# The gate products of a gated linear attention stage, four row groups at once instead of two and two

## The chip, the core and the metric

The kernel runs on one core of one Trainium2 chip. A core has five engines with queues of their own: TensorE (PE; its weight loads are shown as PEld), VectorE (DVE), ScalarE (ACT), GpSimd (POOL) and SyncE (SP, which here issues most DMA transfers). TensorE reads SBUF and writes PSUM, which has eight banks of 128 partitions by 512 float32 values. The engines meet at semaphores. The metric is the device time of one execution in microseconds (us); times are medians of several runs.

## The reference

For 16 batch entries of 256 tokens with 256 features, four layers are added to x one after the other, each on a layernormed x and scaled by the tanh of a scalar gate: a latent cross attention over a context of 77 tokens, a top-2 mixture of experts, a masked cross attention, and the layer that this change is about, a gated linear attention. Cut to what matters here:

```python
q1, k1, v = x @ Wq * scale, x @ Wk, x @ Wv              # 8 heads of 64
q2, k2 = x @ Wqa @ Wqb * scale, softmax(x @ Wka @ Wkb)
gk1 = log_sigmoid(x @ Wg1a @ Wg1b + bg1) / 16           # log decays, per token and feature
gk2 = log_sigmoid(x @ Wg2a @ Wg2b + bg2) / 16
e = softmax(x @ We); idx = top_1(e)                     # 4 experts
o = chunk_gla(q1, k1, v, gk1) + sum over experts of chunk_gla(q2 * e, k2 * e, v, gk2 * mask)
o = o * rsqrt(mean(o * o) + eps) * norm_w * silu(x @ Wga @ Wgb)
out = x + tanh(g_ffn[1]) * (o @ Wo)
```

The two log decays gk1 and gk2 come from products with a contracted dimension of 17 only: 16 low-rank features and a row of ones for the bias.

## The kernel before

The kernel computes everything in float32. Its first two stages (the cross attentions and the experts) are not touched. The last stage, `stage3_fast` (L1530), holds the work of a block, one batch entry b of 256 tokens in two halves of 128 (`tokens(i)`), in four steps, one for each pair of heads: step p belongs to block p // 4, and m = p % 4 is the pair. The order of instructions is written out by hand; after the first part of the stage each engine runs its instructions in program order. The loop (L1905) runs 64 steps, and in each:

- `shares` (den: sums of the second keys' exponentials, on PE into a general bank), `masked(p - 1, 1)` (DVE: four multiplications of the second score product of the step before), `gated` in odd steps (DVE, u), `shares_end` (DVE reads den: `second`, then the reciprocal kden),
- `keys_queries(p + 1)` (PE, kq: keys first, tile wk, then queries, tile wq),
- the tables `middle` and `rest` (what else is due in this step, mostly for the next block), then `decays(p + 1)` (PE gq and gz, ACT ee), then the table `late`,
- `products(p, 0)` (PE, the first score product: sc from f), `masked(p, 0)` (DVE, at from sc and amask), `factors` (DVE, f), the table `by_rows`, `second(p + 1)` (PE, the other halves of gq and gz; ACT, e2), `factors_second` (POOL k, DVE q), the table `logs`,
- `products(p, 1)` (PE, the second score product: sc from q and k) and `values(p - 1)` (PE, o).

A general bank comes from `bank(name)` (L1540): in the loop it is a rotation of two PSUM banks, so a tile waits until the readers of the tile two requests earlier are done. The score products have a tile of two banks to themselves, sc, and only one such tile: the second product of a step waits until DVE has masked the first.

For the next block b + 1, step 0 has `lows` (L1588; PE into a general bank, then two DVE operations make low, whose partitions 64 to 80 and 96 to 112 hold the 17 rows for the two gates), `route_logits` (rt) and, for its own block, `outgates` (zg, with DVE's copy zs in `outgates_end`). Steps 1 and 2 have `gates(b + 1, 0)` and `gates(b + 1, 1)` (L1631): for one half of the tokens two products, out of 17 rows at partitions 64 and 96, each into a general bank, and two Exp by ACT. So they stand between the two score products of their step. `gate_logs` makes the logarithm and `steepest` a maximum for a later check; `decays` reads the result lg four steps on. `scaled` (ms on PE, Ln and Exp on ACT, oT on POOL) normalizes the finished half of the block before, and `project` (proj) in step 2 multiplies it with Wo.

In the profile all matrix products of this stage have line L1548, all transposes L1551, and all DVE, ACT and POOL operations L50; the tile names tell them apart.

Of the kernel before, what the change touches and what calls it, by code (L numbers as in the profile page):

```python
# [10 lines left out]
F32 = mybir.dt.float32  # L11
I32 = mybir.dt.int32
AF = mybir.ActivationFunctionType
ALU = mybir.AluOpType
# [3 lines left out]
P = 128  # L18
B, S, D = 16, 256, 256
# [4 lines left out]
V_LN1G, V_LN1B, V_LN2G, V_LN2B, V_QB, V_KB, V_NW, V_ONE, V_GATE, V_N = 0, 2, 4, 6, 8, 10, 12, 13, 14, 18  # L24
# [49 lines left out]
def layers(ctx: ExitStack, tc: tile.TileContext, t, out, check):  # L74
    nc = tc.nc
# [6 lines left out]
    def const(name, shape, dtype=F32):  # L82
        return cp.tile(list(shape), dtype, tag=name, name=name)
# [33 lines left out]
    vec = const("vec", [P, V_N])  # L117
# [44 lines left out]
    dve3, act3, pool3 = free = [Pinned(tc, x, False) for x in (nc.vector, nc.scalar, nc.gpsimd)]  # L162
# [622 lines left out]
    def w3_load(name, shape, src=None):  # L785
        x = c3(name, shape)
        src = t[src or name]
        weights.append((x, src if len(src.shape) == len(shape) else src.rearrange("(k p) f -> p k f", p=P)))
        return x
# [3 lines left out]
    lbg = w3_load("lbg", [P, 512])  # L793
# [736 lines left out]
    def stage3_fast(early_bank):  # L1530

        with ExitStack() as sx:
# [3 lines left out]
            def of(b):  # L1536

                return w1 if b % 2 else w0

            def bank(name):  # L1540
                return pss.tile([P, 512], F32, tag="ps", name=name) if pss else early_bank(name)

            def tokens(i):
                return slice(i * P, (i + 1) * P)


            def matmul(*a, **k):
                tc.keep_in_program_order(nc.tensor.matmul(*a, **k))  # L1548
# [3 lines left out]

            halves = w1.tile([P, P], F32, tag="halves", name="halves")
            nc.sync.dma_start(out=halves, in_=t["halves"])
            wo = w1.tile([P, 4, D], F32, tag="wo", name="wo")

            hots = [w1.tile([P, 2, 36], F32, tag=f"hot{n}", name=f"hot{n}") for n in range(2)]
# [3 lines left out]
            xn, xnT, low, lg, hT, em, am = {}, {}, {}, {}, {}, {}, {}  # L1561
# [26 lines left out]
            def lows(b):  # L1588

                low[b] = of(b).tile([P, 2, S], F32, tag="low", name="low")  # L1590
                ps = bank("low")
                for c in range(2):
                    for k in range(2):
                        matmul(ps[:, c * S:(c + 1) * S], la[:, k, c * P:(c + 1) * P], xnT[b][:, k, :],
                                         start=k == 0, stop=k == 1)
                dve3.tensor_copy(low[b][:, 0, :], ps[:, :S])
                dve3.tensor_scalar(low[b][:, 1, :], ps[:, S:], vec[:, V_ONE:V_ONE + 1], None, ALU.add)

            e_, den_, z_ = {}, {}, {}

# [30 lines left out]
            def gates(b, i):  # L1631

                if i == 0:
                    lg[b] = of(b).tile([P, 2, 2, 512], F32, tag="lg", name="lg")
                for n, (lo, hi) in enumerate(((64, 81), (96, 113))):
                    ps = bank("z")
                    matmul(ps, low[b][lo:hi, 1, tokens(i)], lbg[lo:hi, :], start=True, stop=True)
                    act3.activation(lg[b][:, i, n, :], ps, AF.Exp, scale=-1.0)

            def gate_logs(b, i):  # L1640
                act3.activation(lg[b][:, i], lg[b][:, i], AF.Ln, bias=1.0)
# [57 lines left out]
            def place(p):  # L1699
                b, m = p // 4, p % 4  # L1700
                return b, m, slice(m * P, (m + 1) * P)

            ee, kq, gq, gz, e2, fq, fk, rd, at, o = {}, {}, {}, {}, {}, {}, {}, {}, {}, {}

            def keys_queries(p):
                b, m, cols = place(p)
                kq[p] = psu.tile([P, 512], F32, tag="kq", name="kq")
                for w, lo in ((wk3, 0), (wq3, S)):
                    for k in range(2):
                        matmul(kq[p][:, lo:lo + S], w[:, k, cols], xnT[b][:, k, :],  # L1710
                                         start=k == 0, stop=k == 1)
# [21 lines left out]
            def shares(p):  # L1733

                ps = bank("den")
                for i in range(2):
                    matmul(ps[:, 2 * i:2 * i + 2], e2[p][:, tokens(i)], halves[:, 0::64],
                                     start=True, stop=True)
                z_[p, "den"] = ps

            def shares_end(p):
                ps = z_.pop((p, "den"))
                rd[p] = st.tile([P, 4], F32, tag="kden", name="kden")
                dve3.tensor_tensor(check["second"], check["second"], ps[:, :4], ALU.max)
                dve3.reciprocal(rd[p], ps[:, :4])
                pool3.tensor_tensor(check["rsum"][:, :4], check["rsum"][:, :4], rd[p], ALU.add)
# [27 lines left out]
            def masked(p, n):  # L1774
                b, m, cols = place(p)
                ps = z_.pop((p, n, "sc"))
                a = w2.tile([P, 2, 384], F32, tag=f"at{n}", name=f"at{n}")
                if n == 0:
                    at[p] = a
                    dve3.tensor_tensor(a, ps[:, :, :384], bc(amask, [P, 2, 384], 1), ALU.mult)  # L1780
                else:
                    r = rd.pop(p)
                    for lo, hi, i in ((0, S, 0), (S, 3 * P, 1)):
                        for j in range(2):
                            dve3.scalar_tensor_tensor(a[:, j, lo:hi], ps[:, j, lo:hi], r[:, 2 * i + j:2 * i + j + 1],
                                                           am[b][:, lo:hi], ALU.mult, ALU.mult)
                    if p == last - 1:
                        at[p] = a
                        return
                    pool3.tensor_tensor(at[p], at[p], a, ALU.add)  # L1790
# [25 lines left out]
            def gated(b, mp):  # L1816
                ps = z_.pop((b, mp, "o"))
                dve3.tensor_tensor(u_[b][:, 2 * mp:2 * mp + 2, :].rearrange("p m s -> p (m s)"), ps,
                                        gw[b][:, 2 * mp:2 * mp + 2, :].rearrange("p m s -> p (m s)"), ALU.mult)
# [36 lines left out]
            def warm():  # L1856

                ps = bank("warm")
                for _ in range(2):
# [2 lines left out]

            start = {0: [(turn, 1)], 2: [(turn_hot, 1)]}
            copies = {2: [(turned_hot, 1)]}
            middle = {0: [(lows, 1)], 1: [(scaled, -1, 1)], 2: [(pairs, 1)], 3: [(scaled, 0, 0)]}

            rest = {0: [(bias, 2)], 1: [(route, 1)], 2: [(steepest, 1, 0), (stats, 2)], 3: [(steepest, 1, 1)]}
            late = {2: [(project, -1)], 3: [(vals, 1)]}
            behind_mask = {0: [(route_logits, 1)], 3: [(norm, 2)]}
            by_rows = {0: [(outgates, 0, 0)], 1: [(gates, 1, 0)], 2: [(gates, 1, 1)], 3: [(outgates, 0, 1)]}  # L1870
            logs = {0: [(route_sums, 1), (outgates_end, 0, 0)], 1: [(gate_logs, 1, 0)], 2: [(gate_logs, 1, 1)],
                    3: [(outgates_end, 0, 1)]}

            def run(steps, p):
                for f, d, *a in steps.get(p % 4, ()):
                    if 0 <= p // 4 + d < B:
                        f(p // 4 + d, *a)
# [16 lines left out]
            w1 = sx.enter_context(tc.tile_pool(name="f3w1", bufs=1, reuse_waits="tile"))  # L1894
            w2 = sx.enter_context(tc.tile_pool(name="f3w2", bufs=2, reuse_waits="tile"))
            psa = sx.enter_context(tc.tile_pool(name="f3psa", bufs=1, space=PSUM, reuse_waits="tile"))
# [8 lines left out]
            for p in range(last):  # L1905
                run(start, p)
                shares(p)
                if 0 < p:
                    masked(p - 1, 1)
                run(copies, p)  # L1910
                if 1 < p and p % 2 == 1:
                    gated((p - 2) // 4, (p - 2) % 4 // 2)
                shares_end(p)
                if p + 1 < last:
                    keys_queries(p + 1)
                run(middle, p)
                run(rest, p)
                if p + 1 < last:
                    decays(p + 1)
                run(late, p)  # L1920
                products(p, 0)
                masked(p, 0)
                run(behind_mask, p)
                if p + 1 < last:
                    factors(p + 1)
                run(by_rows, p)
                if p + 1 < last:
                    second(p + 1)
                    factors_second(p + 1)
                run(logs, p)  # L1930
                products(p, 1)
                if 0 < p:
                    values(p - 1)
                    if p % 2 == 0:
                        squares((p - 1) // 4, (p - 1) % 4 // 2)

            b, p = B - 1, last - 1
# [126 lines left out]
```

## Time and profile before

| | |
|---|---|
| runs | 1928.58, 1929.67, 1936.73 us; median 1929.67 |
| profiled execution | 1930.67 us, of which the span from the first to the last instruction is 1928.8 |
| granted TensorE clock | 0.998 of full speed |
| gate products (z), both token halves, 16 blocks | 128 records, median 588 ns, from 1249.3 to 1865.1 us |
| Exp of a gate (ACT, 128x512) | 64, median 593 ns |
| last stage's loop, one block | 40.70 us |

In the timeline a row gives start, duration, engine, line, operation, the tiles out<-in, the shape, and how many instructions are merged in it; in brackets stands how long the engine was idle before and what ended that. A float32 product shows two records. Records of different row groups of the array overlap, and a record's duration has a tail in which the next one already runs, so how long a product holds PE is read from start to start.

### The profile page before, as it was taken

The numbers are of one execution on the slowest core, as the hardware profiler recorded it, in microseconds if no ns is written. First come the engines' busy times: TensorE is split into PE (matmuls) and PEld (weight loads), VectorE is DVE, ScalarE is ACT, GpSimd is POOL, SyncE is SP. The second block draws the span as 40 slices with busy tenths as digits, with TensorE's granted clock in tenths as the row PEclk, the third lists the DMA queues.
The fourth block names the chain that finished last, engine by engine and source line by source line (L and its number), as shares of the span: only waits on it lengthen the run. The fifth ranks groups of instructions, "written<-read, shape, count | busy, mean of one in ns | idle before, by whom it ended". The sixth has DMA issues, their size and how long they took to land.

```text
span 1928.8 us, 34998 instructions
## 1 busy us (share of the span) xinstructions
PE 1901.3 (99%) x14028; PEld 1323.0 (69%) x14028; DVE 1091.0 (57%) x2637; ACT 870.4 (45%) x1803; POOL 993.5 (52%) x895
## 2 busy tenths in 40 slices
PE   8999999999999999999999999999999999999997
PEld 5666666666766667666787766667777777777775
DVE  3335555455554555544474488865666656666654
ACT  3433334443444434443343588744444444444442
POOL 3644756557565575755635656124444444444433
PEclk9999999999999999999999999999999999999999
DMA  9300000000000000000078733000000000000000
GB/s 337 140 1 3 14 11 14 7 11 14 11 14 9 8 14 9 12 10 9 12 250 250 191 49 49 5 1 6 7 7 6 12 6 7 6 6 7 12 7 14
DMA packets 54028, 75.04 MB, mean 39 GB/s; under 512 B 10096, under 2 KB 43744, under 8 KB 53344
## 3 DMA queue, kind: packets, MB, share of 16 engines
q1 hardware_dynamic: 41568, 55.92, 8.6%
q0 software_dynamic: 12288, 16.79, 4.3%
q8 instruction: 113, 1.85, 0.4%
q14 instruction: 59, 0.48, 0.1%
HBM read 39.14 MB, written 33.55 MB: 38 GB/s over the span
## 4 chain that ended last, share of the span: by engine, by line
PE 95%; DVE 2%; ACT 1%; POOL 1%; issue 0%; DMA 0%; SPq 0%; ACTq 0%; POOLq 0%; DVEq 0%
PE o L50 13%; PE qk L50 13%; PE sc L50 10%; PE v L50 9%; PE proj L50 7%; PE kq L1548 6%; PE sc L1548 5%; PE ex L50 3%; PE gq L1548 3%; PE v L1548 3%; PE proj L1548 3%; PE o L1548 3%; PE gz L1548 2%; PE z L1548 2%; PE den L1548 1%; PE low L1548 1%
## 5 line engine op out<-in xcount | busy, mean ns | idle before, releaser
L50 POOL TENSOR_SCALAR rs<-mv 128x2 f32<-128x2 f32 (+1 forms) x92 | 17.6, 191 | 463.5 <-DVE mv L50 459.8
L50 ACT ACTIVATE qk<-qk 128x256 f32<-128x256 f32 x128 | 49.3, 385 | 343.7 <-PE qk L50 343.6
L50 ACT ACTIVATE e<-sc 111x1024 f32<-111x1024 f32 x192 | 182.2, 1021 | 16.9 <-PE sc L50 16.9
L50 PE MATMUL sc<-qk 64*111 64x256 f32 x1536 | 182.2, 383 | 0.0
L50 PE MATMUL o<-e,v 111*32 111x256 f32 x3072 | 177.5, 379 | 0.0
L50 PE MATMUL v<-wkv,kvT 128*111 128x512 f32 x384 | 169.3, 597 | 0.6 <-DVE kvT L50 0.6
L50 DVE RECIPROCAL rd<-o 128x256 f32<-128x256 f32 x64 | 112.3, 1755 | 99.7 <-PE o L50 99.7
L50 PEld LDWEIGHTS sc<-qk 64*111 64x111 f32 x1536 | 132.1, 172 | 52.9 <-issue 29.0
L50 POOL TENSOR_TENSOR esum<-esum,es 111x512 f32<-111x512 f32 x128 | 163.0, 1274 | 10.0
L50 PE MATMUL qk<-kvT,wkv 128*128 128x333 f32 x512 | 164.3, 443 | 0.0
L50 POOL TENSOR_TENSOR es<-e 111x1024 f32<-111x1024 f32 x64 | 151.2, 2363 | 23.9 <-ACT e L50 22.7
L50 POOL TENSOR_TENSOR k<-e,ee 128x256 f32<-128x256 f32 x64 | 46.8, 732 | 221.9 <-ACT e L50 221.9
L50 POOL TENSOR_TENSOR es<-es,e 111x1024 f32<-111x1024 f32 x64 | 150.4, 2349 | 5.0
L50 PEld LDWEIGHTS o<-e,v 111*32 111x32 f32 x3072 | 99.8, 110 | 66.0
L50 DVE COPY qk<-qk 128x333 f32<-128x333 f32 x128 | 64.6, 504 | 124.5 <-ACT qk L50 123.0
L50 PE MATMUL qk<-kvT,wq 128*128 128x256 f32 x512 | 134.3, 385 | 0.0
L50 PEld LDWEIGHTS v<-wkv,kvT 128*111 128x111 f32 x384 | 67.1, 178 | 91.6 <-issue 90.1
L50 DVE TENSOR_TENSOR at<-sc,amask 128x768 f32<-128x768 f32 x64 | 61.3, 957 | 115.9 <-PE sc L1548 100.6
L50 POOL TENSOR_TENSOR at<-at,at 128x768 f32<-128x768 f32 x63 | 113.9, 1808 | 25.0 <-DVE at L50 15.2
L50 POOL DMA_INDIRECT x<-rows_out,pos x64 | 100.1, 1564 | 37.3 <-issue 15.7
L50 PEld LDWEIGHTS qk<-kvT,wkv 128*128 128x128 f32 x512 | 97.2, 190 | 30.0
L50 PEld LDWEIGHTS qk<-kvT,wq 128*128 128x128 f32 x512 | 94.3, 189 | 34.0 <-issue 13.2
(247 smaller groups left out, 4128.8 us busy)
## 6 DMA issues: line engine op xcount, KB each, us to landing
rows<-zero SPq DMA_DIRECT2D x16, 640.0 KB
xin<-rows SPq DMA_DIRECT2D x16, 640.0 KB
rows_out<-y SPq DMA_DIRECT2D x16, 384.0 KB
x<-in_x_dram SPq DMA_DIRECT2D x16, 256.0 KB
rows_out<-y SPq DMA_DIRECT2D x16, 256.0 KB
out_dram<-x SPq DMA_DIRECT2D x15, 256.0 KB
wkv<-in_wkv_dram SPq DMA_DIRECT2D x2, 1024.0 KB
ew<-in_ew_dram SPq DMA_DIRECT2D x2, 1024.0 KB
```

Source lines behind the costliest of these rows:

```text
L50: x = getattr(self.engine, name)(*a, **k)
L1548: tc.keep_in_program_order(nc.tensor.matmul(*a, **k))
```

## The change

The two products of a half and those of the other half are issued together, for the next block, in step 1, between the key half and the query half of `keys_queries(p + 1)`. To have all four in different groups of 32 rows, the second half of the tokens gets a copy of its rows at partitions 0 to 16 and 32 to 48 (`low2`, two DVE operations in `lows`) and a copy of the gate weights there (`lbg2`, one more DMA at the stage's start). The first half's two products go into two general banks, the second half's two into the sc tile. ACT makes an Exp of the first general bank, then one of both sc banks at once; the Exp of the second general bank (`gates_end`) follows in the table `by_rows`, where `gates` was. Step 2 has no gates any more. `scaled(-1, 1)` moves in step 1 from `middle` to `late`, so behind the decays.

```diff
+            lbg2 = w1.tile([64, 512], F32, tag="lbg2", name="lbg2")
+            nc.sync.dma_start(out=lbg2, in_=t["lbg"][64:P, :])
+            low2 = w1.tile([64, P], F32, tag="low2", name="low2")
...
                 dve3.tensor_scalar(low[b][:, 1, :], ps[:, S:], vec[:, V_ONE:V_ONE + 1], None, ALU.add)
+                if b > 0:
+                    for r in range(0, 64, 32):
+                        dve3.tensor_scalar(low2[r:r + 32, :], ps[64 + r:96 + r, S + P:],
+                                           vec[64 + r:96 + r, V_ONE:V_ONE + 1], None, ALU.add)
...
+            def all_gates(b):
+
+                lg[b] = of(b).tile([P, 2, 2, 512], F32, tag="lg", name="lg")
+                two = psa.tile([P, 2, 512], F32, tag="sc", name="sc")
+                one = [bank("z"), bank("z")]
+                for i in range(2):
+                    for n, (lo, hi) in enumerate(((0, 17), (32, 49))):
+                        x, w = (low2[lo:hi, :], lbg2[lo:hi, :]) if i else (low[b][64 + lo:64 + hi, 1, tokens(0)],
+                                                                         lbg[64 + lo:64 + hi, :])
+                        matmul(two[:, n, :] if i else one[n], x, w, start=True, stop=True)
+                act3.activation(lg[b][:, 0, 0, :], one[0], AF.Exp, scale=-1.0)
+                act3.activation(lg[b][:, 1], two, AF.Exp, scale=-1.0)
+                return one[1]
+
+            def gates_end(b):
+                act3.activation(lg[b][:, 0, 1, :], z_.pop((b, "z")), AF.Exp, scale=-1.0)
...
-            def keys_queries(p):
+            def keys_queries(p, between=None):
...
                 for w, lo in ((wk3, 0), (wq3, S)):
+                    if lo and between is not None:
+                        z_[between, "z"] = all_gates(between)
                     for k in range(2):
...
-            middle = {0: [(lows, 1)], 1: [(scaled, -1, 1)], 2: [(pairs, 1)], 3: [(scaled, 0, 0)]}
+            middle = {0: [(lows, 1)], 2: [(pairs, 1)], 3: [(scaled, 0, 0)]}
...
-            late = {2: [(project, -1)], 3: [(vals, 1)]}
+            late = {1: [(scaled, -1, 1)], 2: [(project, -1)], 3: [(vals, 1)]}
...
-            by_rows = {0: [(outgates, 0, 0)], 1: [(gates, 1, 0)], 2: [(gates, 1, 1)], 3: [(outgates, 0, 1)]}
+            by_rows = {0: [(outgates, 0, 0)], 1: [(gates_end, 1)], 3: [(outgates, 0, 1)]}
...
-                    keys_queries(p + 1)
+                    keys_queries(p + 1, p // 4 + 1 if p % 4 == 1 and p // 4 + 1 < B else None)
```

The first block's gates, made ahead of the loop, stay as they were.

## The prediction

> **What bounds the kernel now.** I read the page first. TensorE's matmuls fill the span and no other engine passes 57%:
>
> ```profile
> PE 1901.3 (99%) x14028; PEld 1323.0 (69%) x14028; DVE 1091.0 (57%) x2637; ACT 870.4 (45%) x1803; POOL 993.5 (52%) x895
> ```
>
> That is an average, and a matmul's shown time includes its tail, so the question is what ends each wait around the edit. The chain of waits of the last stage repeats every 40.70 us (the den of block step 0 starts at 1595.11, and its next at 1635.81) and is all PE. So I read the timeline of one such period, steps 0 and 1 of one block:
>
> ```profile
> 1600.07 0.92 PE L1548 MATMUL sc<-f 64*128 64x256 f32 x8
> ...
> 1601.11 0.96 DVE L50 TENSOR_TENSOR at<-sc,amask 128x768 f32<-128x768 f32 x1 [1.01 <-PE rt L1551]
> ...
> 1602.19 0.76 PEld L1548 LDWEIGHTS sc<-q,k 64*128 64x128 f32 x8 [0.30 <-issue]
> 1602.22 0.92 PE L1548 MATMUL sc<-q,k 64*128 64x256 f32 x8
> ...
> 1603.07 0.87 PE L1548 MATMUL o<-at,v 128*64 128x256 f32 x8
> ...
> 1603.46 0.67 DVE L50 COPY zs<-zg 128x512 f32<-128x512 f32 x1
> ...
> 1604.05 1.39 DVE L50 SCALAR_TENSOR_TENSOR at<-sc,kden,am 128x256 f32<-128x256 f32 x4
> ...
> 1604.34 1.11 PE L1548 MATMUL kq<-xnT,wk 128*128 128x256 f32 x4
> ...
> 1605.29 1.03 PE L1548 MATMUL kq<-xnT,wq 128*128 128x256 f32 x4
> 1605.35 0.68 DVE L50 TENSOR_TENSOR u<-o,gw 128x512 f32<-128x512 f32 x1
> ...
> 1606.01 0.18 DVE L50 RECIPROCAL kden<-den 128x4 f32<-128x4 f32 x1
> ...
> 1607.99 0.92 PE L1548 MATMUL sc<-f 64*128 64x256 f32 x8
> ...
> 1608.85 1.13 PE L1548 MATMUL z<-lbg,low 17*128 17x512 f32 x4
> 1609.03 0.96 DVE L50 TENSOR_TENSOR at<-sc,amask 128x768 f32<-128x768 f32 x1 [0.18 <-PE sc L1548]
> ...
> 1609.90 0.48 PE L1548 MATMUL gq<-low,lbk 64*128 64x256 f32 x1
> ...
> 1610.44 0.82 PE L1548 MATMUL sc<-q,k 64*128 64x256 f32 x8
> ...
> 1611.19 0.87 PE L1548 MATMUL o<-at,v 128*64 128x256 f32 x8
> ```
>
> Step 2 of the same block, in the next stretch of the timeline:
>
> ```profile
> 1619.89 0.92 PE L1548 MATMUL sc<-f 64*128 64x256 f32 x8
> ...
> 1622.39 0.82 PE L1548 MATMUL sc<-q,k 64*128 64x256 f32 x8
> ...
> 1623.14 0.87 PE L1548 MATMUL o<-at,v 128*64 128x256 f32 x8
> ```
>
> And, for four row groups at once, a stretch where the stages overlap:
>
> ```profile
> 1245.29 1.10 PE L50 MATMUL sc<-qT,kd 32*77 32x256 f32 x16
> ```
>
> To be seen here:
> - Between the two score products of a step (sc from f, then sc from q,k) stands the DVE's mask of the first, since both use the one pair of sc banks. In step 0 the mask ends at 1601.11 + 0.96 = 1602.07 and the second product starts at 1602.22, 0.15 later; its weight load had stood 0.30 idle. So step 0 needs 2.15 from product to product although PE has less work than that.
> - In steps 1 and 2 the two gates (z) fill this stretch: 2.45 and 2.50.
> - A product after a wait shows 0.92, one that follows on shows 0.82: a restart costs 0.10.
> - From the first score product to o: 3.00 in step 0 (1603.07 - 1600.07), 3.20 in step 1, 3.25 in step 2.
> - In step 1 the key half of kq hands over to the query half at 1605.29, while DVE reads den only until 1606.01 + 0.18 = 1606.19.
>
> **The change part by part.**
>
> *Removed: the pair of gates in steps 1 and 2.* One pair costs PE 1609.90 - 1608.85 = 1.05 on the chain. But what is left between the score products is the mask's 2.15, as in step 0, so each step only falls from 3.20 and 3.25 to 3.00: 0.20 + 0.25 = 0.45 us a block. Bounds: 0 (DVE later than now), and 2 x 1.05 = 2.10 if the mask gated nothing. I take 0.45; step 0 is the same code with the mask on the path.
>
> *Added: four gate matmuls between the halves of kq of step 1.* Their work: the 8 records of kq, 256 columns each, take 1.83 on the chain, 0.23 each, so the 16 records of the 32-row product would take 3.7 one by one; they stand in 1.10, so four row groups do run at once. Four gates together thus cost about what two do: 1.05, and 0.10 because the query half then starts cold: 1.15.
>
> Their waits: gate tiles come from bank(), a rotation of two banks. The requests of step 0 are den, low, rt, zg, then den in step 1; so the first gate gets zg's bank (free when DVE's zs copy ends, 1603.46 + 0.67 = 1604.13, early enough), and the second gets den's, which is free only when shares_end has made kden. That is 1606.19, behind masked (1604.05 to 1605.44) and gated (u, to 1606.03) on DVE's queue, 0.90 after the key half is done. The other two want the sc pair, free when masked ends, earlier on that same queue. PE is in order: the first gate runs alone, the other three start at 1606.19 + 0.15 = 1606.34. Nothing of the waiting is used. The query half starts at 1606.34 + 1.05 = 1607.39 instead of 1605.29, and cold: 2.10 + 0.10 = **2.20 us a block**. Behind the waiting gate are queued the query half, the decays, ms and everything after; DVE, ACT and POOL wait for those, so nothing overtakes. Bounds: 1.15 (no wait), and 3.05 if the last two gates don't overlap the second (two more passes, 0.86, as the 512-column ms occupies on the chain). The DVE chain from the mask of step 0 to kden (1601.11 to 1606.19) is back to back and starts from a PE event, so the 0.90 returns every block: the extra time on PE comes after it.
>
> *low2: two DVE ops of 32x128 a block, in step 0.* Not in the trace; the 128x256 form beside it takes 0.47 (1599.63), so the two cost at most 0.94; at least 0.3, twice the smallest op near it (second, 128x4, 0.15). They start at 1600.10; the mask of step 0 had DVE waiting 1.01 before 1601.11, which covers them. They also hold the low bank, whose next user zg started at 1600.83: up to 0.3 late, covered by the 0.30 that PE idles ahead of 1602.19. Zero; every 0.1 that showed would be 1.5 in all.
>
> *ACT.* Four Exp of 128x512 (0.593 each) become two, one of 128x1024 (the same-sized Ln takes 1.07), and one, late: 2.25 instead of 2.37. The Exp that frees the sc pair ends near 1607.39 + 0.2 + 1.07 = 1608.7; the next score product comes at 1607.99 + 2.20 = 1610.19, behind query half, decays and ms. Covered by 1.5. gates_end holds den's former bank until about 1612.3; the next taker, hT, stood at 1611.99 and moves to about 1613.9. Covered.
>
> *scaled, moved behind the decays.* The same ms (0.86), Ln, Exp and POOL's oT; the ee of the next step no longer queue behind Ln and Exp. oT was ready at 1609.99 and is used by proj at 1616.34; it comes some 3 us later, proj 2 later: covered. Zero.
>
> *One DMA more,* lbg2, 128 KB on SP, ahead of the gp loads, used much later: 128 KB at the 250 GB/s that the page shows in the stage transition is 0.5 us, at most that.
>
> *Sum.* 15 of the 16 blocks prepare a next one. 2.20 - 0.45 = 1.75 each; in the first the DVE is 0.12 nearer, and its step 1 gains some more from the wait: take 1.4. 14 x 1.75 + 1.4 = 25.9, call it +26. The profiled execution took 1930.67 (span 1928.8), so 1956.7; it stands 1.0 over the median of the three runs, 1929.67, so the median becomes **1955.7**.
>
> The Trainium skill, "TensorEngine Tiling (Array Packing)", section Theoretical Speedup, gives up to 4x for a contracted dimension of 32 or less; by that rule alone one pair's time goes away in every block, 15 x 1.05 = 16 us, and as an estimate the kernel would take 1914. The same page's PSUM Bottleneck speaks against: tiling speeds TensorE, not the emptying of PSUM, and after the speedup the latter may become the limit. The rows above are of that kind (the mask's 2.15, kden's 0.90), and they decide.
>
> **The rivals.**
> 1. *Slower, but the den bank doesn't gate* (some other order of banks, or DVE early). For: the wait is worked out from the rotation, not seen. Against: DVE's rows are back to back. 15 x (1.15 - 0.45) = +10.5: 1940.
> 2. *The four gates run two by two.* For: sc here is a pair of banks of one tile. Against: 16 records in 1.10. 15 x (3.05 - 0.45) = +39: 1969.
> 3. *Faster: the mask gates nothing,* so both removed pairs are saved whole: 15 x (1.15 - 2.10) = -14: 1915. It needs the mask to be done when gq and gz are, 0.85 + 0.54 = 1.39 after the score product instead of 2.15; with the wait for kden it breaks even once removal is worth 2.20 a block. Against: the mask alone is 0.96 and starts 1.04 after the product does; steps 0 and 3 have 2.15 in every block.
> 4. *No effect:* the insertion falls into a hole of PE. There is none: the halves of kq adjoin.
>
> **How the numbers follow.** Main case 0.80 (1950 to 1961: insertion 2.0 to 2.4, removal 0.3 to 0.5), rival 1 0.08, rival 2 0.06, rival 3 0.03, no effect 0.03. The range takes in the main case and most of rival 1 towards it: 1943 to 1963. About 0.5% (10 us) is what a measurement can tell from no change: slower 0.93, same 0.04, faster 0.03.
>
> **What would show it.** Right: in step 1 the second z starts some 1.0 after the key half, just behind kden; kq's two halves lie some 2.2 further apart; f to q,k product is 2.15 in all four steps; the period grows from 40.70 to about 42.45. Wrong: z matmuls that start right behind the key half, score products closer than 2.1, or DVE idle in step 0 gone (low2 too long).

## The result, and the profile after

| | before | after |
|---|---|---|
| median of four runs each, us | 1930.70 (1928.58 to 1936.73) | 1961.08 (1960.43 to 1966.83) |
| profiled execution, us (span) | 1930.67 (1928.8) | 1960.43 (1958.6) |
| one block of the loop, us | 40.70 | 42.45 |
| first den of the loop to the last, us | 634.26 | 659.11 |
| start of the loop's first den, us | 1270.81 | 1276.06 |

The change makes the kernel slower by 1.6%: the ratio is 1.0159, 95% interval 1.0129 to 1.0189. Two places hold the 29.8 us between the profiled executions: the loop, +24.85, and what lies ahead of it, +5.25; the part behind the loop is 0.3 shorter. The profile of before has 3.4 us of half TensorE clock in the first step of its loop and the one of after has none there; without them the loop's part would be about +26.5 (see the part on the sum below).

The page of the kernel after, engines' busy time. PE has the same 14028 instructions, and a smaller share:

```profile
PE 1904.8 (97%) x14028; PEld 1318.9 (67%) x14028; DVE 1098.2 (56%) x2667; ACT 874.1 (45%) x1788; POOL 992.7 (51%) x895
```

The timeline of the kernel after, step 1 of a block (start, duration, engine, operation, tiles; idle before and what ended it in brackets). Here and below rows that don't bear on the reading are left out, also where no dots stand:

```profile
1621.58 1.39 DVE L50 SCALAR_TENSOR_TENSOR at<-sc,kden,am 128x256 f32<-128x256 f32 x4
1621.88 1.11 PE L1548 MATMUL kq<-xnT,wk 128*128 128x256 f32 x4
...
1622.88 0.68 DVE L50 TENSOR_TENSOR u<-o,gw 128x512 f32<-128x512 f32 x1
1622.92 1.61 PE L1548 MATMUL z<-lbg,low 17*128 17x512 f32 x3
1623.54 0.17 DVE L50 RECIPROCAL kden<-den 128x4 f32<-128x4 f32 x1
1623.87 0.70 PE L1548 MATMUL sc<-lbg,low 17*128 17x512 f32 x2
1624.93 1.13 PE L1548 MATMUL kq<-xnT,wq 128*128 128x256 f32 x4
1625.04 1.02 ACT L50 ACTIVATE lg<-sc 128x1024 f32<-128x1024 f32 x1 [0.37 <-PE sc L1548]
...
1627.74 0.92 PE L1548 MATMUL sc<-f 64*128 64x256 f32 x8
1628.78 0.96 DVE L50 TENSOR_TENSOR at<-sc,amask 128x768 f32<-128x768 f32 x1 [2.40 <-PE sc L1548]
1629.88 0.92 PE L1548 MATMUL sc<-q,k 64*128 64x256 f32 x8 [0.79 <-DVE at L50]
1630.74 0.87 PE L1548 MATMUL o<-at,v 128*64 128x256 f32 x8
```

The first gate starts right behind the key half (1622.92). The other three stand until kden ends (1623.54 + 0.17 = 1623.71) and start at 1623.87. Then all three are through in 1.06, when the query half starts (1624.93): three row groups do run at once, but behind a wait, and the first gate runs ahead of them alone. Further down, PE now idles 0.79 for the mask where the pair of gates used to be, and f to o takes 3.00 (1630.74 - 1627.74) instead of 3.20.

Step 2 of the same block, PE's rows:

```profile
1639.43 0.92 PE L1548 MATMUL sc<-f 64*128 64x256 f32 x8
...
1641.58 0.92 PE L1548 MATMUL sc<-q,k 64*128 64x256 f32 x8 [0.79 <-DVE at L50]
1642.43 0.87 PE L1548 MATMUL o<-at,v 128*64 128x256 f32 x8
```

2.15 from score product to score product, and 3.00 to o instead of 3.25: the mask's time, as in step 0 before. And in step 0, DVE:

```profile
1617.17 1.22 DVE L50 TENSOR_SCALAR low<-low,vec 128x256 f32<-128x256 f32 x3
...
1618.65 0.96 DVE L50 TENSOR_TENSOR at<-sc,amask 128x768 f32<-128x768 f32 x1 [0.26 <-PE rt L1551]
```

The two low2 operations add 0.75 (1.22 for three, 0.47 for the one before), and DVE's wait ahead of the mask falls from 1.01 to 0.26. It still waits, so they cost nothing.

### The profile page after: what moved, and what is told of

The parts are those of the page before. It is cut to its first block, busy times and chain, and to the rows that moved or that the text cites. A ratio compares the mean times of both kernels' runs of the same rounds, so it can differ in the third digit from the quotient of the medians.

```text
span 1958.6 us, 35015 instructions
## 1 busy us (share of the span) xinstructions
PE 1904.8 (97%) x14028; PEld 1318.9 (67%) x14028; DVE 1098.2 (56%) x2667; ACT 874.1 (45%) x1788; POOL 992.7 (51%) x895
## 4 chain that ended last, share of the span: by engine, by line
PE 93%; DVE 3%; ACT 1%; DMA 1%; issue 1%; POOL 1%; SPq 0%; DVEq 0%; ACTq 0%; POOLq 0%
PE o L50 13%; PE qk L50 13%; PE sc L50 10%; PE v L50 9%; PE proj L50 7%; PE kq L1548 6%; PE sc L1548 6%; PE ex L50 3%; PE v L1548 3%; PE proj L1548 3%; PE o L1548 3%; PE gq L1548 2%; PE gz L1548 2%; DVE at L50 2%; PE z L1548 2%; PE den L1548 1%
```

## Experiments on what the insertion costs

The theory is the prediction's: 2.20 us a block go to the four gates, of which about one is the wait for kden. Two kernels shorten that wait in different ways, one to nothing and one by the greater part. The first issues the gates behind the query half:

```diff
                 for w, lo in ((wk3, 0), (wq3, S)):
-                    if lo and between is not None:
-                        z_[between, "z"] = all_gates(between)
                     for k in range(2):
...
+                if between is not None:
+                    z_[between, "z"] = all_gates(between)
```

> The changed kernel with the four gate products behind both halves of kq instead of between them. Theory A (the wait for kden is what makes the insertion dear): the query half (0.86) now covers most of the 0.90, so the wait falls from 1.05 to about 0.2; the period falls from 42.45 to 41.6, the time by 15 x 0.85 = 13 to 1948. Rival B (the four products are dear in themselves, for a change of the array's row grouping or for the score pair's banks): no change, 1961, period 42.4 or more.

Measured: 1947.28 (1946.29 to 1948.64), ratio to before 1.0085 [1.0068, 1.0101], a block 41.59. Its timeline, step 1:

```profile
1616.81 1.03 PE L1548 MATMUL kq<-xnT,wq 128*128 128x256 f32 x4
1617.53 0.17 DVE L50 RECIPROCAL kden<-den 128x4 f32<-128x4 f32 x1
1617.77 0.74 PE L1548 MATMUL z<-lbg,low 17*128 17x512 f32 x2
1617.86 0.70 PE L1548 MATMUL sc<-lbg,low 17*128 17x512 f32 x2
1618.92 0.71 PE L1548 MATMUL gq<-dmask,lg 128*128 128x128 f32 x4
```

kden is done before the query half is, all four gates start within 0.09, and gq follows 1.15 behind the first. Against a query half that is followed at once (0.86 to the next product), the gates also start 0.10 late (0.96), and gq to gz takes 0.11 longer: an insertion without any wait costs 0.10 + 1.15 + 0.11 = 1.36, not the 2.20 with it. The block agrees: 40.70 - 0.45 + 1.36 = 41.61.

The second leaves the gates where the change put them and gives DVE the other order, so that den is read ahead of u in step 1:

```diff
+                if p % 4 == 1:
+                    shares_end(p)
                 if 1 < p and p % 2 == 1:
                     gated((p - 2) // 4, (p - 2) % 4 // 2)
-                shares_end(p)
+                if p % 4 != 1:
+                    shares_end(p)
```

> The changed kernel with DVE's order swapped in step 1: den is read and kden made before u, not behind it. Theory A (the second gate waits for kden): kden comes 0.67 earlier, so do the three gates, and the period falls from 42.45 to 41.8, the time by 15 x 0.67 = 10 to 1951. Rival B (the gates wait for the mask of the score banks, or for something on ACT): no change, 1961.

Measured: 1951.79 (1950.20 to 1956.19), ratio 1.0107 [1.0090, 1.0124], a block 41.86. Its timeline:

```profile
1622.29 1.01 PE L1548 MATMUL z<-lbg,low 17*128 17x512 f32 x2
1622.31 0.18 DVE L50 RECIPROCAL kden<-den 128x4 f32<-128x4 f32 x1
...
1622.64 0.70 PE L1548 MATMUL sc<-lbg,low 17*128 17x512 f32 x2
1623.70 1.13 PE L1548 MATMUL kq<-xnT,wq 128*128 128x256 f32 x4
```

With one DVE operation of 0.68 out of the way the other gates follow the first after 0.35 instead of 0.95, and 0.59 a block comes back. So the wait for den's bank is the cause, shown from both sides, and its price is what DVE still has to do ahead of kden.

## Experiments on what the removal is worth

The prediction gave only 0.45 a block for the two pairs taken out from between the score products, since the mask holds the stretch at 2.15. The rival says a whole pair, 1.05, each time. Here the kernel before leaves out the second pair, and the decays read the first half's gates for both:

```diff
                     lg[b] = of(b).tile([P, 2, 2, 512], F32, tag="lg", name="lg")
+                elif b > 0:
+                    return
...
-                act3.activation(lg[b][:, i], lg[b][:, i], AF.Ln, bias=1.0)
+                act3.activation(lg[b][:, i], lg[b][:, 0 if b else i], AF.Ln, bias=1.0)
...
-                        matmul(ps[:, tokens(i)], lg[b][:, i, n, cols], mask[:, i, :], start=True, stop=True)
+                        matmul(ps[:, tokens(i)], lg[b][:, 0 if b else i, n, cols], mask[:, i, :], start=True, stop=True)
```

> The kernel before, without the gate products and Exp of the second token half in step 2: the decays read the first half's for both, so this part of the computation is left out. Theory A (what the removal is worth is bounded by the DVE mask between the two score products): step 2 from the first score product to o falls from 3.25 to 3.00, the period from 40.70 to 40.45, the time by 15 x 0.25 = 4 to 1926. Rival B (a pair of gates is worth its PE time): 15 x 1.05 = 16 less, 1914, period 39.65.

Measured: 1927.50 (1923.32 to 1931.46, ten runs) beside 1931.42, ratio 0.9981 [0.9970, 0.9992], a block 40.44. Its timeline, step 2:

```profile
1617.89 0.92 PE L1548 MATMUL sc<-f 64*128 64x256 f32 x8
...
1618.93 0.96 DVE L50 TENSOR_TENSOR at<-sc,amask 128x768 f32<-128x768 f32 x1 [0.18 <-PE sc L1548]
...
1620.04 0.92 PE L1548 MATMUL sc<-q,k 64*128 64x256 f32 x8 [0.79 <-DVE at L50]
1620.89 0.87 PE L1548 MATMUL o<-at,v 128*64 128x256 f32 x8
```

Work of 1.05 is gone, and 0.25 comes back (3.25 to 3.00). The rest has become PE's wait for the mask. DVE itself had waited 0.18 for the product when it began the mask (1618.93), so it could not start sooner.

If what sticks out over the mask is all there is to gain, then shortening the pairs in their place should win it too. The next kernel is the kernel before with the gates two and two as before, in a 64-row form: the 17 rows stand in a 64-row tile that is zero elsewhere (lbgz), and the second gate's x rows are copied to partitions 0 to 63 (low2), so that the gates share the row grouping of the score products around them:

```diff
+            lbgz = w1.tile([P, 512], F32, tag="lbgz", name="lbgz")
+            pool3.memset(lbgz, 0.0)
+            low2 = w1.tile([64, S], F32, tag="low2", name="low2")
...
+                if b > 0:
+                    dve3.tensor_scalar(low2, ps[64:P, S:], vec[64:P, V_ONE:V_ONE + 1], None, ALU.add)
...
-                    matmul(ps, low[b][lo:hi, 1, tokens(i)], lbg[lo:hi, :], start=True, stop=True)
+                    if b == 0:
+                        matmul(ps, low[b][lo:hi, 1, tokens(i)], lbg[lo:hi, :], start=True, stop=True)
+                    elif n == 0:
+                        matmul(ps, low[b][64:P, 1, tokens(i)], lbgz[64:P, :], start=True, stop=True)
+                    else:
+                        matmul(ps, low2[:, tokens(i)], lbgz[0:64, :], start=True, stop=True)
...
+            nc.sync.dma_start(out=lbgz[64:81, :], in_=t["lbg"][64:81, :])
+            nc.sync.dma_start(out=lbgz[32:49, :], in_=t["lbg"][96:113, :])
```

> The kernel before, its gates left two and two in steps 1 and 2, but in the 64-row form of the products around them: the two gate weights stand in a zero-filled tile, one in the upper, one in the lower 64 rows, and low2 is a copy of 64 rows. No change of row grouping is left between the two score products. Theory A (a pair of gates costs only what it exceeds the mask's 2.15 by, and that is the two changes of grouping): steps 1 and 2 fall from 3.20 and 3.25 to 3.00, the period from 40.70 to 40.25, the time by 15 x 0.45 = 7, from 1931 to 1924: faster than both kernels. Rival B (64 rows cost a pair more, or DVE's copy comes late): 1931 or more.

Measured: 1928.75 (1926.60 to 1934.60, twelve runs) beside 1932.13, ratio 0.9984 [0.9971, 0.9997], a block 40.38. Its timeline, step 1:

```profile
1607.27 0.92 PE L1548 MATMUL sc<-f 64*128 64x256 f32 x8
1608.02 1.03 PE L1548 MATMUL z<-lbgz,low 64*128 64x512 f32 x4
...
1608.52 0.18 PEld L1548 LDWEIGHTS gq<-low,lbk 64*128 64x128 f32 x1 [0.30 <-ACT ee L50]
...
1608.88 0.38 PE L1548 MATMUL gq<-low,lbk 64*128 64x256 f32 x1
1609.07 0.48 PE L1548 MATMUL gz<-low,lbk 64*128 64x256 f32 x1
1609.41 1.01 PE L1548 MATMUL sc<-q,k 64*128 64x256 f32 x8
1610.35 0.87 PE L1548 MATMUL o<-at,v 128*64 128x256 f32 x8
```

z follows the score product after 0.75 instead of 0.86, and the pair is through in 0.86 (1608.88 - 1608.02) instead of 1.05: with one row grouping throughout, the delay at the change of grouping is gone. 0.32 of the 0.45 a block arrives, 0.20 of it in step 2. f to o is 3.08 here, not 3.00: one of the second products (gq, gz) waited for ACT's ee, and the two row groups went on out of step.

## Experiments on the moved step

`scaled` was moved behind the decays, at a price of zero in the prediction. Alone, in the kernel before:

```diff
-            middle = {0: [(lows, 1)], 1: [(scaled, -1, 1)], 2: [(pairs, 1)], 3: [(scaled, 0, 0)]}
+            middle = {0: [(lows, 1)], 2: [(pairs, 1)], 3: [(scaled, 0, 0)]}
...
-            late = {2: [(project, -1)], 3: [(vals, 1)]}
+            late = {1: [(scaled, -1, 1)], 2: [(project, -1)], 3: [(vals, 1)]}
```

> The kernel before with one part of the change alone: scaled(-1, 1) behind the decays in step 1. Theory A (it is worth nothing, as its cost in the prediction: PE does the same work on the same path): period 40.70, 1931 within 1.5. Rival B (oT late for proj, or f late because PE reaches the score product no later while ee now comes sooner): a period more than 0.1 off.

Measured: 1934.25 (1930.56 to 1940.58, ten runs) beside 1934.07, ratio 1.0007 [0.9988, 1.0026], a block 40.78. Its timeline, step 1:

```profile
1608.45 0.92 PE L1548 MATMUL sc<-f 64*128 64x256 f32 x8
1608.56 0.69 ACT L50 ACTIVATE r<-ms,eps 128x512 f32<-128x512 f32 x1
1609.30 1.21 PE L1548 MATMUL z<-lbg,low 17*128 17x512 f32 x4
```

Nothing in the time, but 0.08 in the block: with ms moved, a gate behind it takes ms's bank, and ACT's Ln reads that until 1609.25 (the row r<-ms). The z records stand in 1.21 instead of 1.13. In the changed kernel no gate is behind ms any more, and its block grew by 1.75 = 2.20 - 0.45, which leaves nothing for the move.

The same move in the 64-row kernel should take its gates off the wait for ee:

```diff
-            middle = {0: [(lows, 1)], 1: [(scaled, -1, 1)], 2: [(pairs, 1)], 3: [(scaled, 0, 0)]}
+            middle = {0: [(lows, 1)], 2: [(pairs, 1)], 3: [(scaled, 0, 0)]}
...
-            late = {2: [(project, -1)], 3: [(vals, 1)]}
+            late = {1: [(scaled, -1, 1)], 2: [(project, -1)], 3: [(vals, 1)]}
```

> The gates in the 64-row form, two and two, and scaled(-1, 1) behind the decays as in the change. In the 64-row form alone step 1 kept 3.08 instead of 3.00, since gz of the second half waited for ACT's ee, which stands behind ms's Ln and Exp. Theory A (that queue is the cause): step 1 falls to 3.00, the period from 40.38 to 40.30, the time by 1.2 from 1928.7 to 1927.5. Rival B (the wait is for something else): step 1 stays at 3.08 and the period at 40.38.

Measured: 1928.43 (1924.92 to 1937.29, twelve runs) beside 1934.07, ratio 0.9974 [0.9959, 0.9989], a block 40.38 and 3.08 in step 1, both as without the move. Its timeline, step 1:

```profile
1617.02 0.69 ACT L50 ACTIVATE r<-ms,eps 128x512 f32<-128x512 f32 x1
1617.67 1.30 PE L1548 MATMUL z<-lbgz,low 64*128 64x512 f32 x4
```

The wait for ee went and the wait for ms's bank came: ee is done by the time the score product starts (1616.91), but z's records stand in 1.30 instead of 1.03 and begin (1617.67) while ACT still reads ms (until 1617.71). So theory A falls, and the wait is another one, as rival B says. This kernel and the 64-row kernel without the move are a little faster than before (0.2 to 0.3%, intervals below 1) and the only two here that do all of the work and beat both; which of the two is better the intervals don't tell.

Last, in the kernel with the gates behind the query half, `scaled` goes between the score products of step 1, where PE now waits for the mask:

```diff
-            late = {1: [(scaled, -1, 1)], 2: [(project, -1)], 3: [(vals, 1)]}
+            late = {2: [(project, -1)], 3: [(vals, 1)]}
...
-            by_rows = {0: [(outgates, 0, 0)], 1: [(gates_end, 1)], 3: [(outgates, 0, 1)]}
+            by_rows = {0: [(outgates, 0, 0)], 1: [(gates_end, 1), (scaled, -1, 1)], 3: [(outgates, 0, 1)]}
```

> The four gates behind both halves of kq, and the product ms of step 1 moved between the two score products, where taking the gates away left PE idle for 0.79. Theory A (the removal was worth so little because PE now waits there for the mask): ms goes off the path where it was (0.86) and there exceeds the mask's 2.15 by 0.3 with two changes of row grouping, so the period falls by 0.55 from 41.6 to 41.05, the time by 8 from 1947 to 1939. Rival B (the hole can't take work, since the next product waits for ms's bank or for ACT): 1947 or more.

Measured: 1945.35 (1943.39 to 1946.68, five runs) beside 1932.13, ratio 1.0062 [1.0041, 1.0084], a block 41.42: 0.17 of the 0.55 that was expected. Its timeline, step 1:

```profile
1618.92 1.02 ACT L50 ACTIVATE lg<-sc 128x1024 f32<-128x1024 f32 x1
...
1619.99 0.92 PE L1548 MATMUL sc<-f 64*128 64x256 f32 x8 [0.41 <-ACT lg L50]
1620.84 1.12 PE L1548 MATMUL ms<-sq,halves 128*128 128x512 f32 x2
...
1622.43 0.82 PE L1548 MATMUL sc<-q,k 64*128 64x256 f32 x8
1623.18 0.87 PE L1548 MATMUL o<-at,v 128*64 128x256 f32 x8
```

The ms product fits between, nearly (3.19 to o instead of 3.00), but it had been the cover of ACT's Exp of the sc pair. Without it the score product waits 0.41 for that Exp (1618.92 + 1.02 = 1619.94): a wait that ms had hidden where it stood comes up as soon as its cover goes.

## Experiments on the five microseconds ahead of the loop

The prediction allowed 0.5 us at most for the load of lbg2 ahead of the gp loads, where stage 2 hands over to its second half. But the loop starts 5.25 later. PE's waits in the timeline of the kernel after, at that place, with ACT's copy of the first gp:

```profile
1098.86 0.37 ACT L50 COPY gpx<-gp 77x256 f32<-77x256 f32 x1 [2.83 <-DMA gp<-in_gpT_dram]
...
1100.62 0.63 PE L50 MATMUL o<-pg,vd 77*32 77x256 f32 x4 [3.44 <-DVE pg L50]
```

and of the kernel before:

```profile
1096.74 0.37 ACT L50 COPY gpx<-gp 77x256 f32<-77x256 f32 x1 [0.61 <-DMA gp<-in_gpT_dram]
...
1098.51 0.63 PE L50 MATMUL o<-pg,vd 77*32 77x256 f32 x4 [1.22 <-DVE pg L50]
```

gp lands 2.1 later, PE idles for 3.44 rather than 1.22, and a stretch of half TensorE clock follows. A window of the kernel after (time, length, busy time and instructions of PE, PEld, DVE, ACT and POOL, granted clock, share and rate of the DMA engines); the kernel before has a clock of 1.00 there:

```profile
1100.00:1110.00 10.00, 8.96 (x84) 4.06 (x84) 6.46 (x12) 6.52 (x11) 1.37 (x4) 0.66 0.15 25
```

A granted clock of 0.66 over 10 us is 6.8 us at half speed, which loses up to 3.4; with the 2.1 of gpx that is up to 5.5, enough for the 5.25. The first suspect is the load itself; it moves down in the program:

```diff
-            nc.sync.dma_start(out=lbg2, in_=t["lbg"][64:P, :])
...
+            nc.sync.dma_start(out=lbg2, in_=t["lbg"][64:P, :])
             psu = sx.enter_context(tc.tile_pool(name="f3psu", bufs=1, space=PSUM, side="right", reuse_waits="tile"))
```

> The changed kernel with only the load of lbg2 issued later, behind the gp loads of the second stage. Theory A (the load on SP's queue ahead of gp delays the first gp by 2.1 us, and the PE then idles 3.4 us and loses 3 more to a half clock): the 5.3 us that the loop does not explain go away, 1961 becomes 1956; the loop's period stays 42.45. Rival B (the 5.3 us come from elsewhere at the hand-over of the stages, the gathers or the placing of tiles): within 1 us of 1961.

Measured: 1960.88 (1955.75 to 1966.85), ratio 1.0154 [1.0124, 1.0184]. But the edit did less than it says. SP's rows in its profile:

```profile
1093.32 1.47 SPq L1214 DMA_DIRECT2D gp<-in_gpT_dram  x3
1094.83 0.56 SPq L1914 DMA_DIRECT2D lbg<-in_lbg_dram  x1
```

SP issued the load behind three gp loads and not behind the stage, 1.5 later than in the changed kernel counted from the load of halves: it still ran beside them. So this run doesn't tell. Both kernels once more, to see what differs from execution to execution:

> The changed kernel once more, line for line, for a second profile of it. Open is where its start of the loop, 5.26 us later than before (the first den at 1276.06 instead of 1270.81), comes from: gpx stands 2.12 later and 6.8 us of half clock follow. Theory A, the change does it: gpx within 0.3 of 1098.86 and the first den within 1 of 1276.1. Theory B, it differs from execution to execution, whatever the kernel: gpx or the first den moves by over 1 us and the half-clock stretch has another place or length. Both: a period of 42.45, and from the first den to the last 659.1.

> The changed kernel a third time, line for line. A: gpx at 1098.9 and the first den at 1276.1, as in the first profile and in the second. B: one of them more than 1 us from the other profiles of the same kernel, with the half-clock stretches elsewhere.

> The kernel before once more, line for line. A: gpx at 1096.74 and the first den at 1270.8, within 0.3 and 1. B: more than 1 us from these in one of the two; the half-clock stretches, one of 3.4 at 1272.4 in the first profile, stand elsewhere. Both: a period of 40.70.

Measured: 1962.25 (1962.11 to 1963.77) for the changed kernel again, ratio 1.0147 [1.0121, 1.0173]; single executions of 1962.91 and, for the kernel before, 1928.31. What their profiles show, with two kernels from above that keep the first part of before, and one more that follows below:

| profile | gpx, us | gpx behind halves' issue | half clock at the hand-over | first den |
|---|---|---|---|---|
| before | 1096.74 | 4.32 | none | 1270.8 |
| before, again | 1094.21 | 3.96 | none | 1269.1 |
| before without the second half's gates | 1096.69 | 4.31 | 3.4 | 1272.3 |
| before with `scaled` moved | 1096.78 | 4.23 | 3.4 | 1272.4 |
| after | 1098.86 | 6.54 | 6.8 | 1276.1 |
| after, again | 1099.33 | 5.05 | 3.4 | 1275.6 |
| after, third | 1096.67 | 5.89 | 17.1 | 1277.9 |
| after, lbg2 copied | 1096.07 | 5.58 | 13.7 | 1276.7 |

Neither theory is right as it stood. The pieces do move by over 1 us between executions of one kernel (gpx by 2.7, the half-clock stretch from 3.4 to 17.1), but the sum goes with the kernel: the first den comes 4.8 to 8.7 later in the three executions of the changed kernel than in the two of before. Over all profiles, it lies at 1269.1 to 1272.4 in the four with the first part of before and at 1275.1 to 1278.6 in the eight with that of the change, 5.5 later on average. So something in the changed kernel and not chance costs about five us there, though a single pair of profiles can show 3 or 9. (The two 64-row kernels, with other tiles, have 1272.3 and 1280.6.) The load had still not been excluded. The last kernel has no such load: DVE copies lbg's rows in SBUF, just ahead of the loop.

```diff
-            nc.sync.dma_start(out=lbg2, in_=t["lbg"][64:P, :])
...
+            dve3.tensor_copy(lbg2, lbg[64:P, :])
             dve3.tensor_scalar(wo, wo3, vec[:, V_NW:V_NW + 1], None, ALU.mult)
```

> The changed kernel without its one more transfer: lbg2 is a copy of lbg's rows that DVE makes in SBUF, where the changed kernel loads it from DRAM. In five profiles in which a 128 KB load of lbg2 stands among the gp loads, the wait of PE for the first pg there is 1.8 to 3.8 us in all, and gpx starts 4.9 to 6.5 after the issue of halves; in four without it 0.4 to 1.6, and 4.0 to 4.3. The run that put the load later in the program did not take it away from there: SP issued it 0.9 later, behind three gp loads instead of in front of them. Theory A, the load delays gp, PE idles longer, and half clock follows: gpx 4.0 to 4.4 behind halves, PE's wait under 1.7, the first den near 1271; the loop as in the changed kernel, period 42.45; the time 1930.7 + 24.9 = 1955.6, 1954 to 1958. Theory B, something else in the first part costs the five us: 1961, with gpx at most as much nearer as the wait.

Measured: 1960.57 (1959.17 to 1962.15) beside 1929.89, ratio 1.0145 [1.0120, 1.0169]. (Two figures of that expectation were miscounted: the profiles with the load are seven, and the move in the earlier run was 1.5.) SP's row for halves, and ACT's for gpx:

```profile
1090.49 0.33 SPq L1554 DMA_DIRECT2D halves<-in_halves_dram  x1
```

```profile
1096.07 0.37 ACT L50 COPY gpx<-gp 77x256 f32<-77x256 f32 x1 [1.86 <-DMA gp<-in_gpT_dram]
```

No lbg2 load stands there, gpx still comes 5.58 behind halves, and the first den is at 1276.7. So the load is not what delays the hand-over: theory A falls. What does is open. Nor is it shown that the half clock follows from the late gp: one 64-row kernel has 13.7 us of it there with gpx 4.33 behind halves and no wait of PE above 0.8, and two kernels with the first part of before have 3.4 after waits of 1.1 and 1.2. The kernels that keep the first part of before (the two profiles of before, the one without the second half, the one with `scaled` moved) have gpx 3.96 to 4.32 behind halves; those with the change's lbg2 and low2 have 4.90 to 6.54, eight of eight; the two 64-row kernels, with other tiles, have 4.64 and 4.33. The edits common to the eight in this part are the two tiles in w1, which may shift what is placed behind them; that was not tried.

## Why the prediction was right, and where it was not

The forecast was 1955.7 in a range of 1943 to 1963; 1961.1 was measured, the main case came, at its upper edge, and every rival failed. The mechanism was right in the loop. That the total stayed inside is in part luck: about five us came from a place that the prediction had put at 0.5 at most, and the range happened to have room for them.

- **Insertion, 2.20.** Right to 0.01: from where the query half would have started (1621.88 + 0.95) to where it did (1624.93) are 2.10, and 0.10 for the cold start. Its parts were right too: kden done 0.90 after the key half (0.88: 1623.71 - 1622.83), the second gate 1.05 after it (1.04), the last three together in 1.05 (1.06). The two kernels with the wait gone and shortened show the cause.
- **Its lower bound, 1.15.** Too low: without a wait it is 1.36, since the entrance costs 0.10 too and the four gates take 1.15 and not 1.05. Rival 1 would have been 15 x (1.36 - 0.45) = +13.7, not +10.5. The wait was there, so this decided nothing.
- **Removal, 0.45.** 0.20 + 0.25, measured in both steps, and 0.25 by itself in the kernel without the second half.
- **low2, ACT, scaled: zero.** low2 took 0.75 of DVE's 1.01; the Exp of the sc pair ended at 1626.06 with the next score product at 1627.74, a cover of 1.7 (1.5 predicted), of which ms behind the decays makes about one (0.95, from 1626.79). In the kernel with the gates behind the query half there is less of it, and the run with `scaled` between the products shows the wait. `scaled` is zero in the changed kernel, though 0.08 a block in the kernel before, by the bank.
- **The sum over blocks, 25.9.** 24.85 between first and last den: 1.75 in a steady block, as predicted. The first block had +1.4 in the prediction, and its step 1, from den to den, takes 1.34 more (9.31 instead of 7.97). But the block as a whole is 0.36 shorter, since its step 0 takes 9.30 instead of 10.99. That is the clock of before's profile and not the change, as the windows of before and after show (the columns are those of the window above):

```profile
1270.00:1280.00 10.00, 9.09 (x49) 7.48 (x49) 4.71 (x10) 2.18 (x6) 2.15 (x3) 0.83 0.00 0
```

```profile
1270.00:1280.00 10.00, 8.20 (x47) 6.32 (x46) 7.18 (x17) 2.18 (x6) 2.88 (x5) 1.00 0.00 0
```

0.83 over 10 us is 3.4 us at half clock, a loss of 1.7. The two kernels with before's step 0 and no half clock there take 9.31 for it. At full clock the loop thus grows by about 26.5, the sum of the prediction and 0.6 from two single steps, whose cause is open.
- **The load, at most 0.5.** This term failed. Not by the load, which the last run acquits, but because the prediction looked for the cost of the edits ahead of the loop in their instructions alone. 5.25 us came there, as a later gp and a stretch of half clock, by a cause that is open. Between the profiled executions 26.5 in the loop, less the 1.7 of before's half clock, plus 5.25, less 0.3 at the end is the 29.8 measured, 3.8 over the forecast's 26. The median is 5.4 over its forecast: the forecast put it 1.0 under the profiled execution, and it lies 0.65 over.
- **Rival 2** (two by two) is excluded by the 1.06 for three gates; **rival 3** (the mask gates nothing) by the 0.79 of waiting for `at` in steps 1 and 2; **rival 4** by the period.

The estimate by the 4x rule of the Trainium skill, "TensorEngine Tiling (Array Packing)", 1914, misses by 47. Its PSUM Bottleneck section fits the runs: the array did four products in 1.15 (two took 1.05), and the time was set by who reads the banks (0.79 of waiting for the mask, 0.95 for kden).

## What to carry to other kernels

Work taken from between two products that a reader of PSUM holds apart is worth only what sticks out over that reader (0.20 and 0.25 of 1.05 here), so it is read from a step that lacks the work, not from the work's length. Work put where PE is without holes costs its whole length and, with tiles from a rotation, whatever the last reader of the bank still has queued ahead of it: find that reader's place on its engine first. And a stage that an edit hardly touches can come out slower (five us here, as much as three blocks of the loop lost, by a cause that stayed open), so read the hand-over of the stages in both traces before the loop gets all the blame.

## What the hardware showed beyond this

- **Half clock came in steps of 3.4 us.** Every such stretch in the middle of the fourteen traces has a length of 3.4, 6.8, 13.7 or 17.1, at half the clock. The Trainium skill, "TensorE: Matmul & The Clock Gate", Part 1, has a window of about 3.4 us and half speed after an idle window; the lengths agree. But the hole did not have to be one window long here: the changed kernel had 6.8 us after a hole of 3.44, in its third profile 17.1 us began within one of 2.78, and one 64-row kernel had 13.7 behind waits of 0.8 and less.
- **A change of row grouping has a price.** About 0.1 on the way in and 0.1 on the way out at float32 (z after the score product 0.86, and 0.75 in the 64-row form; gq to gz 0.55 behind the gates instead of 0.44). For a pair of 1.05 that is a fifth, and giving it the neighbours' grouping paid for it without moving anything. Whether the 17 rows themselves have a part in it was not tried.
- **Row groups can go on out of step.** In the 64-row kernels one of gq and gz starts 0.2 to 0.3 behind the other, where one row group had waited (for ee in the one kernel, for ms's bank in the other), and o, behind them, comes 0.08 later (3.08 for 3.00).
